# Lead of the first attention stage: fillers in halves between the half-steps, and the first shift of q built in the eleventh step in the fillers' PSUM

## Chip, cores and metric

The kernel runs on one core of a Trainium2 chip. The metric is the device time of one execution in microseconds (us); lower is better. All arithmetic is in f32. In the profiles one f32 matmul of the program shows as two hardware passes ("x8" for four matmuls), and so it is counted here.

## The reference, cut to what matters

The program is a block of an adaptive transformer: a 16-head attention with a gate and a position field, a soft mixture of 64 experts, and two layers of local attention and gated feed-forward. The change touches only the beginning of the first part, on x of shape (2, 1024, 256):

```python
def _L0_cond_ref(x, consciousness_state, ...):
    qkv = (x @ Wqkv.T + bqkv).reshape(Bb, Ss, 3, H, HD).transpose(2, 0, 3, 1, 4)   # H=16 heads of HD=16
    q, k, v = (qkv[0], qkv[1], qkv[2])
    attn = jax.nn.softmax(jnp.einsum('bhid,bhjd->bhij', q, k) / jnp.sqrt(jnp.float32(HD)), axis=-1)
    coh = jax.nn.sigmoid(jnp.tanh(comb @ Wc1.T + bc1) @ Wc2.T + bc2).transpose(0, 2, 1)
    mod = attn * coh[..., None]
    mod = mod / (mod.sum(-1, keepdims=True) + 1e-08)
    fp = _layernorm(jax.nn.relu(consciousness_state @ We1.T + be1) @ We2.T + be2, ln_g, ln_b)
    fa = jax.nn.softmax(jnp.einsum('be,se->bs', fp, pe), axis=-1)
    mod = (1.0 - fi) * mod + fi * fa[:, None, :, None]
    out = jnp.einsum('bhij,bhjd->bhid', mod, v).transpose(0, 2, 1, 3).reshape(Bb, Ss, Ee)
    return out @ Wout.T + bout
```

`comb` is x with the 64 state values joined to it. The softmax over the keys needs a maximum for each query and head before the exponentials.

## The kernel before, in words

The first attention is cut into eight units, each one batch and four heads. Each head has its own strip of 32 partitions (16 for the head, one more for the shift by the maximum), so that one matmul of a head contracts over 32 rows of TensorE's array and the four heads of a unit lie on its four row strips. A unit has 16 steps.

`maxima(step, half)` (L286 to L302) serves one block of 128 queries and one half of 512 keys for two of the four heads: two matmuls (L295; four passes of "32*128 32x512") write a PSUM tile `pm` of 128x1024, and VectorE reduces it to two maxima per query (L302). `half` 0 uses the row strips 0 and 1, `half` 1 the strips 2 and 3. `pm` comes from `wide`, a PSUM pool of two tiles, so a `pm` must wait until the reduction two half-steps earlier has read its tile. `largest(hu)` (L304) joins the two key halves of eight steps; `shift(hu)` (L308) transposes these maxima into PSUM (`pmx`, four transposes at L313) and adds them to q on VectorE, which gives `qs` (L317). `score` (L329) multiplies `qs` with the keys, and ScalarE takes the exponentials (L337).

The maxima run 12 steps ahead of the scores (`LEAD = 12`). So before the first score there is a lead of 12 steps with maxima alone, written out by hand (L661 to L699) for the queues of TensorE, VectorE and ScalarE: what stands first in the code stands first in each of these queues. To have work for TensorE beside VectorE's reductions, each step of the lead ends with a "filler", some other work of the stage that needs all 128 rows of the array: the input side of the coherence gate (`coherence_in`, L524, tiles `pz`, four passes a step), the values (`values`, L194, `pv`, eight passes of 256 columns), the logits of the field (`field_logits`, L615, `fl`), a rotation matrix (`rotation`, L652, `prot`) and the output of the gate (`coherence_out`, L542, `pc`, column strips of 32). Four very small ones go with them: `field_in`, `field_mean`, `field_var` and `field_out` (tiles `pfp`, `pfm`, `pfv`, `pfac`). [...] VectorE, ScalarE and GpSimd each read the fillers' results in passing.

A step of the lead is `maxima(m, 0)`, `maxima(m, 1)`, then the whole filler. After the twelfth step come `shift(0)`, in the PSUM of the maxima, and then the loop over scores, where each step pairs scores on two strips with maxima on the other two.

Of the kernel before, what the change touches and what calls it, by code (L numbers as in the profile page):

```python
# [17 lines left out]
P = 128  # L18
B = 2
S = 1024  # L20
D = 256
# [42 lines left out]
W_PRO, N_PRO = _layout([("wc1x", D), ("we2", D), ("wc2", 32)])  # L64
# [27 lines left out]
def tile_kernel(ctx: ExitStack, tc: tile.TileContext, a: dict, out: bass.AP):  # L92
    nc = tc.nc
# [24 lines left out]
    rot = res.tile([P, 2, D], F32, name="rot")  # L118
# [56 lines left out]
    def wide(name):  # L175
        return ps_s.tile([P, 2, 512], F32, tag="s", name=name)

    def pair(name):
        return ps_t[0].tile([P, 2, 512], F32, tag="t", name=name)
# [3 lines left out]

    pvs = {}

    def values(b, half, tile, part, lead=False):

        if part == 0:
            pvs[b, half] = tile("pv").rearrange("p x (y d) -> p (x y) d", d=D)
        pt = pvs[b, half]  # L190
        for y in (2 * part, 2 * part + 1):
            j = 4 * half + y
            for k in range(2):
                nc.tensor.matmul(  # L194
                    pt[:, y, :],
                    xT[b][:, k, j * P : (j + 1) * P],
                    watt("wv", k, 0, D),
                    start=(k == 0),
                    stop=(k == 1),
                )  # L200
        if part == 0:
            return
        to = v[b][:, 4 * half : 4 * half + 4, 0 : H0 * VW].rearrange("p j (h d) -> p j h d", d=VW)[
            :, :, :, 0:HD0
        ]
        pt = pt.rearrange("p j (h d) -> p j h d", d=HD0)
        bias = bcast(rows[:, ROWS["bv"]].rearrange("p (h d) -> p h d", d=HD0), 1, 4)
        if lead:
            nc.scalar.copy(to, pt)
            nc.gpsimd.tensor_tensor(to, to, bias, ALU.add)  # L210
        else:
            nc.vector.tensor_tensor(to, pt, bias, ALU.add)
# [66 lines left out]
    def spread(u):  # L279

        for what, dst in (("k", km[u % 3]), ("q", qm[u % 2])):
            for h in range(4):
                r0 = 64 * (u % 2) + HD0 * h
                nc.sync.dma_start(dst[32 * h : 32 * h + HD0, :], heads[what][r0 : r0 + HD0, :])
# [20 lines left out]
        mx2 = mxs.pop(hu)  # L305
        nc.vector.tensor_tensor(mxt[hu % 2][:, :, :, AUG], mx2[:, :, :, 0], mx2[:, :, :, 1], ALU.max)

    def shift(hu):  # L308

        u, n = divmod(hu, 2)  # L310
        pt = wide("pmx")[:, 0, :]
        for i in range(4):
            nc.tensor.transpose(  # L313
                pt[:, i * P : (i + 1) * P], mxt[hu % 2][:, i, :, :].rearrange("p h r -> p (h r)"), ident
            )
        at = slice(n * 512, (n + 1) * 512)
        nc.vector.tensor_tensor(qs[u % 2][:, at], qm[u % 2][:, at], pt, ALU.add)  # L317
# [131 lines left out]
    with tc.tile_pool(name="pro", bufs=1, side="right") as pro:  # L449
        w_cs = pro.tile([CD, N_CS], F32, name="w_cs")  # L450
        nc.gpsimd.dma_start(w_cs, a["w_cs"])
        w_pro = pro.tile([P, 2, N_PRO], F32, name="w_pro")
# [7 lines left out]
        def wsl(w, lay, name, c, lo, n):  # L460
            at = lay[name].start + lo
            return w[:, c, at : at + n]
# [43 lines left out]
        th = {}  # L506
# [8 lines left out]
                nc.vector.tensor_scalar(csb[:, c, :], pt[:, 0, c, :], col("bc1", c), None, ALU.add)  # L515
                nc.vector.tensor_scalar(hid[:, c, :], pt[:, 1, c, :], col("be1", c), 0.0, ALU.add, ALU.max)

        def coherence_in(b, n, c):
            if c == 0:
                th[b, n] = pair("pz")  # L520
            pz = th[b, n]
            t0 = n * 512
            for k in range(2):
                nc.tensor.matmul(  # L524
                    pz[:, c, :],
                    wsl(w_pro, W_PRO, "wc1x", k, c * P, P),
                    xT[b][:, k, t0 : t0 + 512],
                    start=(k == 0),
                    stop=(k == 1),
                )  # L530
            if c == 0:
                return
            th[b, n] = at2.tile([P, 2, 512], F32, tag="e", name="th", bufs=6)
            for c in range(2):
                nc.scalar.activation(th[b, n][:, c, :], pz[:, c, :], AF.Tanh, bias=csb[:, c, b : b + 1])

        def coherence_out():

            pc = pair("pc")[:, 0, :]
            for k in range(2):  # L540
                for g in range(4):
                    nc.tensor.matmul(  # L542
                        pc[32 * g : 32 * g + 32, :],
                        wsl(w_pro, W_PRO, "wc2", k, 0, 32),
                        th[g // 2, g % 2][:, k, :],
                        start=(k == 0),
                        stop=(k == 1),
                    )
            for g in range(4):
                th.pop((g // 2, g % 2))  # L550
            th["out"] = at2.tile([P, 2, 512], F32, tag="e", name="cg", bufs=6)[:, 0, :]
            nc.scalar.copy(th["out"], pc)

# [53 lines left out]
                    fpc[:, c, :], fpc[:, c, :], col("ln_g", c), col("ln_b", c), ALU.mult, ALU.add  # L607
                )

        def field_logits(n):  # L610
            if n == 0:
                th["fl"] = pair("fl")
            fl = th["fl"][0:B]
            for k in range(2):
                nc.tensor.matmul(  # L615
                    fl[:, n, :],
                    fpc[:, k, :],
                    peT[:, k, n * 512 : (n + 1) * 512],
                    start=(k == 0),
                    stop=(k == 1),  # L620
                )
            if n == 0:
                return
            th.pop("fl")
            fmx = pro.tile([B, 1], F32, name="fmx")
            nc.vector.tensor_reduce(fmx, fl.rearrange("p n t -> p (n t)"), AX.X, ALU.max)
            nc.vector.tensor_scalar(fmx, fmx, -1.0, None, ALU.mult)
            fe = at2.tile([P, 2, 512], F32, tag="e", name="fe", bufs=6)[0:B].rearrange("p n t -> p (n t)")
            fsum = pro.tile([B, 1], F32, name="fsum")
            nc.scalar.activation(  # L630
                fe, fl.rearrange("p n t -> p (n t)"), AF.Exp, bias=fmx, accum_out=fsum
            )
            th["fe"] = fe, fsum
# [11 lines left out]
                nc.tensor.transpose(pt[:, i, :], fe[:, i * P : (i + 1) * P], ident[0:B, 0:B])  # L645
            nc.vector.tensor_copy(fac.rearrange("p (b i) -> p i b", b=B), pt)

        def rotation(mats):
            pt = pair("prot")
            for c in range(2):  # L650
                for k in range(2):
                    nc.tensor.matmul(  # L652
                        pt[:, c, :D],
                        mats[0][:, k, c * P : (c + 1) * P],
                        mats[1][:, k, :],
                        start=(k == 0),
                        stop=(k == 1),
                    )
            nc.scalar.copy(rot, pt[:, :, :D])

        with tc.manual_schedule(  # L661
            engines={mybir.EngineType.PE, mybir.EngineType.DVE, mybir.EngineType.Activation}
        ):
            pq, pk = wide("pqk"), wide("pqk")
            for pt, what, n in ((pq, "q", 0), (pk, "k", 0), (pk, "k", 1), (pq, "q", 1)):
                project_part(pt, 0, what, 0, n)
            project_end(pk, "k", 0)
            project_end(pq, "q", 0)
            spread(0)
            from_state()  # L670
            coherence_in(0, 0, 0)
            coherence_in(0, 0, 1)
            values(0, 0, pair, 0, True)
            values(0, 0, pair, 1, True)
            fill = [
                [field_in, lambda: coherence_in(0, 1, 0)],
                [field_mean, lambda: coherence_in(0, 1, 1)],
                [field_var, lambda: values(0, 1, pair, 0, True)],
                [lambda: values(0, 1, pair, 1, True), lambda: spread(1)],
                [lambda: field_logits(0)],  # L680
                [lambda: field_logits(1)],
                [lambda: coherence_in(1, 0, 0)],
                [lambda: coherence_in(1, 0, 1), field_scale],
                [lambda: coherence_in(1, 1, 0)],
                [lambda: coherence_in(1, 1, 1), field_out],
                [lambda: rotation(mats)],
                [coherence_out],
            ]
            mats = None
            for m in range(LEAD):  # L690
                maxima(m, 0)
                maxima(m, 1)
                for f in fill[m]:
                    f()
                if m == 3:
                    mats = matrices()
                if m == 8:
                    largest(0)
            shift(0)  # L699

    def of_banks(bufs):
        banks.close()
# [11 lines left out]
    for u in range(len(units)):  # L714
        if u % 2 == 0 and u + 2 < len(units):
            b, g = units[u + 2]
# [29 lines left out]
    with tc.manual_schedule(  # L746
        engines={mybir.EngineType.PE, mybir.EngineType.DVE, mybir.EngineType.Activation}
    ):
        for s in range(STEPS):
# [11 lines left out]
            m = s + LEAD  # L761
# [204 lines left out]
    y = [mo1.tile([P, NE // 4, D], F32, name="y0"), xp.tile([P, NE // 4, D], F32, tag="y1", name="y1")]  # L966
    dxs = ExitStack()
    dx = dxs.enter_context(tc.tile_pool(name="dx", bufs=2))
    with tc.manual_schedule(
# [5 lines left out]
        for it in range(3, ITS):  # L975
            n, m = divmod(it, 8)
# [6 lines left out]
            i = it - ITS + 8  # L983
# [89 lines left out]
    with tc.manual_schedule(  # L1073
# [250 lines left out]
        def halves(f):  # L1324
            l, b, t0 = chunk(f)
            nc.gpsimd.tensor_tensor(
                fa["sq"][:, 0, :], shifted(xb, 0, b, t0, 512), shifted(xb, 1, b, t0, 512), ALU.add
            )
# [343 lines left out]
```

## Time and profile before

| what | us |
|---|---|
| median of 3 runs (1624.53 to 1625.74) | 1625.15 |
| the profiled execution | 1625.17 |
| its span, first to last instruction | 1623.2 |
| TensorE's busy time in the span | 1591.8 |
| mean granted TensorE clock | 0.999 of full speed |
| the lead: first maxima to first score, from 24.65 to 67.19 | 42.5 |
| one reduction of a `pm` (L302), mean of 256 | 1.220 |

A page of the profile gives busy times per engine and the costliest groups of instructions. Three views go closer. The timeline lists instructions by start, merged where one form follows itself. The chain of waits follows the end of a stretch back, at each step to what released it, so its pieces lie end to end. A table of windows gives each engine's busy time in a stretch. PE is a matmul pass, PEld the loading of its weights, DVE is VectorE, ACT is ScalarE, POOL is GpSimd.

### The profile page before, as it was taken

The page shows a single profiled execution, that of the slowest core. Times are in us where ns is not written, and L with a number is a line of the kernel's source. Part 1 is how long each engine was busy: PE and PEld are TensorE (multiplying, and loading weights), DVE is VectorE, ACT ScalarE, POOL GpSimd, SP SyncE. Part 2 cuts the span into 40 slices and gives each one's busy share as a digit, 9 for nine tenths or more (in the row PEclk, how much of TensorE's full clock was granted, in tenths as well). Part 3 has the DMA queues.
Part 4 walks back from the last instruction along what each step waited for, and adds up shares of the span by engine and source line. Part 5 has one row for each costly group of instructions (what it writes and reads, how often), then busy time and mean ns, then how long its engine had stood idle before and what let it go on. Part 6 is the DMA issues. An engine that isn't in the chain of part 4 may idle for free.

```text
span 1623.2 us, 22628 instructions
## 1 busy us (share of the span) xinstructions
PE 1591.8 (98%) x8660; PEld 803.4 (49%) x8660; DVE 941.9 (58%) x1605; ACT 884.8 (55%) x1653; POOL 538.3 (33%) x830
## 2 busy tenths in 40 slices
PE   8999999999999999999999999999999999999998
PEld 4333333333333444444877676555555555655543
DVE  4768758776763122225446755757576666666632
ACT  2477767777886222235234544656657575656531
POOL 3233323333330100000103434555565555465411
PEclk9999999999999999999999999999999999999999
DMA  5100000010000544546532002000100001000001
GB/s 157 52 14 14 1 16 12 1 21 8 1 1 27 169 141 151 178 148 195 184 126 78 27 1 80 1 1 1 65 1 0 14 1 54 1 6 22 14 14 39
DMA packets 49707, 82.65 MB, mean 51 GB/s; under 512 B 4536, under 2 KB 24928, under 8 KB 49344
## 3 DMA queue, kind: packets, MB, share of 16 engines
q1 hardware_dynamic: 47056, 75.38, 15.0%
q0 software_dynamic: 1584, 5.29, 1.1%
q8 instruction: 68, 1.11, 0.3%
q10 hardware_dynamic: 960, 0.56, 0.1%
q14 instruction: 39, 0.32, 0.1%
HBM read 56.04 MB, written 20.97 MB: 47 GB/s over the span
## 4 chain that ended last, share of the span: by engine, by line
PE 89%; DVE 6%; ACT 2%; POOL 1%; issue 1%; DMA 1%; DVEq 0%; ACTq 0%; POOLq 0%
PE pga L1371 8%; PE sc L329 8%; PE po L347 7%; PE pm L295 7%; PE lg L795 7%; PE sl L821 7%; PE pq L1121 6%; PE cmb L909 5%; PE pwo L1310 3%; PE po L1290 3%; PE sc L1210 3%; PE py L1396 3%; PE pv L1177 3%; PE pe L1271 3%; PE pqk L265 2%; PE py L842 2%
## 5 line engine op out<-in xcount | busy, mean ns | idle before, releaser
L302 DVE TENSOR_REDUCE mx<-pm 128x2 f32<-128x1024 f32 x256 | 302.5, 1220 | 117.9 <-PE pm L295 117.3
L337 ACT ACTIVATE e<-sc 128x512 f32<-128x512 f32 (+1 forms) x500 | 266.2, 611 | 72.2 <-PE pm L295 44.6
L329 PE MATMUL sc<-qs,km 32*128 32x512 f32 x1024 | 254.7, 619 | 0.9 <-DVE qs L317 0.9
L295 PE MATMUL pm<-km,qm 32*128 32x512 f32 x1024 | 246.0, 619 | 2.4 <-ACT xa L432 0.6
L365 POOL TENSOR_TENSOR ob<-ob,part 128x512 f32<-128x512 f32 x101 | 128.4, 1271 | 270.2 <-ACT part L364 270.2
L1227 DVE CUSTOM_DVE_ANT_0 e<-sc,mask,zn 128x256 f32<-128x256 f32 (+1 forms) x256 | 102.3, 463 | 69.5 <-PE sc L1210 69.5
L1371 PE MATMUL pga<-hc,w 128*128 128x512 f32 x320 | 141.1, 593 | 0.0
L1260 POOL TENSOR_SCALAR e<-e,den 128x256 f32<-128x256 f32 (+1 forms) x128 | 131.1, 1038 | 27.0 <-DVE den L1256 27.0
L347 PE MATMUL po<-e,v 128*32 128x512 f32 x1024 | 136.7, 604 | 0.0
L329 PEld LDWEIGHTS sc<-qs,km 32*128 32x128 f32 x1024 | 87.5, 183 | 84.6 <-ACT e L337 64.4
L1244 ACT ACTIVATE e<-e,nmx 128x256 f32<-128x256 f32 (+1 forms) x256 | 123.5, 485 | 1.9 <-DVE nmx L1227 1.6
L1145 POOL TENSOR_TENSOR t<-raw,tabs 128x512 f32<-128x512 f32 x64 | 81.5, 1295 | 124.8 <-ACT raw L1135 119.6
L1121 PE MATMUL pq<-wqo,xa 128*128 128x512 f32 x256 | 115.9, 595 | 1.6 <-DVE xb L897 0.9
L909 PE MATMUL cmb<-xb,y 128*128 128x256 f32 x512 | 116.6, 380 | 0.2 <-ACT xb L895 0.2
L795 PE MATMUL lg<-phi,xa 128*128 128x512 f32 x256 | 115.9, 595 | 0.3 <-ACT xa L432 0.3
L821 PE MATMUL sl<-dsp,xb 128*128 128x512 f32 x256 | 114.9, 592 | 0.0
L295 PEld LDWEIGHTS pm<-km,qm 32*128 32x128 f32 x1024 | 82.8, 183 | 60.0 <-DVE mx L302 31.7
L805 DVE TENSOR_TENSOR l<-lg,keep 128x512 f32<-128x512 f32 x32 | 22.1, 692 | 143.5 <-ACT keep L803 143.5
L909 PEld LDWEIGHTS cmb<-xb,y 128*128 128x128 f32 x512 | 94.9, 190 | 16.6 <-issue 3.2
L1135 ACT COPY raw<-pq 128x1024 f32<-128x1024 f32 x32 | 32.4, 1013 | 128.6 <-PE pq L1121 126.8
L1371 PEld LDWEIGHTS pga<-hc,w 128*128 128x128 f32 x320 | 59.2, 190 | 67.2 <-issue 63.9
L803 ACT COPY keep<-lg 128x512 f32<-128x512 f32 x32 | 18.7, 585 | 125.1 <-issue 107.4
(212 smaller groups left out, 2491.2 us busy)
## 6 DMA issues: line engine op xcount, KB each, us to landing
lgd<-keep SPq DMA_DIRECT2D x64, 256.0 KB, 2.4
w<-in_ffn_W SPq DMA_DIRECT2D x16, 1024.0 KB, 7.5
ebig<-lgd SPq DMA_DIRECT2D x64, 256.0 KB, 3.3
wqo<-in_wqkv SPq DMA_DIRECT2D x2, 1536.0 KB, 8.6
w<-in_w SPq DMA_DIRECT2D x2, 1386.0 KB, 5.9
km<-hk SPq DMA_DIRECT2D x32, 64.0 KB, 2.3
qm<-hq SPq DMA_DIRECT2D x32, 64.0 KB, 2.3
phi<-in_phi SPq DMA_DIRECT2D x1, 2048.0 KB, 7.6
```

The costliest lines, as they stand in the source:

```text
L295: nc.tensor.matmul(pm[:, x, :], qm[u % 2][r, i * P : (i + 1) * P], km[u % 3][r, n * 512 : (n + 1) * 512], start=True, stop=True,)
L302: nc.vector.tensor_reduce(mxs[hu][:, i % 4, 2 * half : 2 * half + 2, n], pm, AX.X, ALU.max)
L329: nc.tensor.matmul(sc[:, x, :] if both else sc[x], km[u % 3][r, j * P : (j + 1) * P], qs[u % 2][r, n * 512 : (n + 1) * 512], start=True, s ...
L337: nc.scalar.activation(part, t, AF.Exp, scale=1.0 / HD0**0.5)
L347: nc.tensor.matmul(po[32 * hh : 32 * hh + 32, :], v[b][:, j, at : at + 32], es[s, hh // 2][:, hh % 2, :], start=True, stop=True,)
L365: nc.gpsimd.tensor_tensor(obs[u, n], obs[u, n], part, ALU.add)
L795: nc.tensor.matmul(lg[:, b, :], xa[:, k, b, 1 + m * P : 1 + (m + 1) * P], phi[:, k, n * 512 : (n + 1) * 512], start=(k == 0), stop=(k == 1),)
L821: nc.tensor.matmul(accs[n][b][:, c, :], xo_tm[:, b * 8 + m, c * P : (c + 1) * P], d[:, b, :], start=(m == 0), stop=(m == 7),)
L909: nc.tensor.matmul(acs[q][:, c, :], y[b][:, 4 * jj + j, c * P : (c + 1) * P], eT[:, j // 2, j % 2 * 256 : (j % 2 + 1) * 256], start=(jj == ...
L1121: nc.tensor.matmul(pq[:, x, :], shifted(xa, k, b, w * WIN, P), load["wqkv"][:, k, x * 512 : (x + 1) * 512], start=(k == 0), stop=(k == 1),)
L1260: engine.tensor_scalar(e[:, x, c, lo:], e[:, x, c, lo:], den[:, x, c : c + 1], None, ALU.mult)
L1371: nc.tensor.matmul(pt[:, x, :], load["w1"][:, k, lo : lo + P], hcs[f][:, k, :], start=(k == 0), stop=(k == 1))
```

## The change

Each filler is cut in two, and a half stands behind each `maxima` of a step: `maxima(m, 0)`, first half, `maxima(m, 1)`, second half. No matmul, reduction or transfer is added or left out. The small fillers stay with the same step: `field_in`, `field_mean` and `field_var` now between the step's first maxima and its first half of filler, `field_out`, `field_scale` and the loads of the second unit behind the second half. `shift(0)` goes from the end of the lead to the end of the eleventh step (index 10) and takes its PSUM tile from `pair`. `coherence_out`, the filler of the last step, keeps its tile in `th["pc"]` between its halves. The queues of SP and GpSimd keep their order; on TensorE and VectorE only the lead changes.

```diff
-    def values(b, half, tile, part, lead=False):
+    def values(b, half, tile, part, lead=False, which=(0, 1)):
...
-        for y in (2 * part, 2 * part + 1):
+        for y in (2 * part + i for i in which):
...
-    def shift(hu):
+    def shift(hu, tile=wide):
...
-        pt = wide("pmx")[:, 0, :]
+        pt = tile("pmx")[:, 0, :]
...
-        def coherence_in(b, n, c):
-            if c == 0:
+        def coherence_in(b, n, c, which=(0, 1)):
+            if c == 0 and 0 in which:
                 th[b, n] = pair("pz")
...
-            for k in range(2):
+            for k in which:
...
-            if c == 0:
+            if c == 0 or 1 not in which:
                 return
...
-        def coherence_out():
-
-            pc = pair("pc")[:, 0, :]
-            for k in range(2):
-                for g in range(4):
+        def coherence_out(k):
+
+            if k == 0:
+                th["pc"] = pair("pc")[:, 0, :]
+            pc = th["pc"]
+            for g in range(4):
...
+            def halves(f, *args):
+                return [lambda y=y: f(*args, (y,)) for y in range(2)]
+
+            def value_halves(half, part):
+                return [lambda y=y: values(0, half, pair, part, True, (y,)) for y in range(2)]
+
             fill = [
...
+                halves(coherence_in, 0, 1, 0),
+                halves(coherence_in, 0, 1, 1),
+                value_halves(1, 0),
+                value_halves(1, 1),
+                halves(field_logits, 0),
+                halves(field_logits, 1),
+                halves(coherence_in, 1, 0, 0),
+                halves(coherence_in, 1, 0, 1),
+                halves(coherence_in, 1, 1, 0),
+                halves(coherence_in, 1, 1, 1),
+                [lambda: rotation(0), lambda: rotation(1)],
+                [lambda: coherence_out(0), lambda: coherence_out(1)],
             ]
-            mats = None
+            also = {
+                (0, 0): field_in,
+                (1, 0): field_mean,
+                (2, 0): field_var,
+                (3, 1): lambda: spread(1),
+                (7, 1): field_scale,
+                (9, 1): field_out,
+                (10, 1): lambda: shift(0, pair),
+            }
             for m in range(LEAD):
-                maxima(m, 0)
-                maxima(m, 1)
-                for f in fill[m]:
-                    f()
+                for y in range(2):
+                    maxima(m, y)
+                    early = (m, y) in ((0, 0), (1, 0), (2, 0))
+                    if early:
+                        also[m, y]()
+                    fill[m][y]()
+                    if (m, y) in also and not early:
+                        also[m, y]()
                 if m == 3:
                     mats = matrices()
                 if m == 8:
                     largest(0)
-            shift(0)
```

`field_logits` and `rotation` are cut in the same way.

More of the change, by code (lines that the diff above doesn't have):

```diff
@@ L184, in tile_kernel @@
     pvs = {}
-    def values(b, half, tile, part, lead=False):
-        if part == 0:
+    def values(b, half, tile, part, lead=False, which=(0, 1)):
+        if part == 0 and 0 in which:
             pvs[b, half] = tile("pv").rearrange("p x (y d) -> p (x y) d", d=D)
         pt = pvs[b, half]
-        for y in (2 * part, 2 * part + 1):
+        for y in (2 * part + i for i in which):
             j = 4 * half + y
@@ L200, in values @@
                 )
-        if part == 0:
+        if part == 0 or which == (0,):
             return
@@ L535, in coherence_in @@
                 nc.scalar.activation(th[b, n][:, c, :], pz[:, c, :], AF.Tanh, bias=csb[:, c, b : b + 1])
-        def coherence_out():
-            pc = pair("pc")[:, 0, :]
-            for k in range(2):
-                for g in range(4):
[L542 to L548, printed above, removed]
+        def coherence_out(k):
[3 more added lines that the diff above has]
+            for g in range(4):
+                nc.tensor.matmul(
+                    pc[32 * g : 32 * g + 32, :],
+                    wsl(w_pro, W_PRO, "wc2", k, 0, 32),
+                    th[g // 2, g % 2][:, k, :],
+                    start=(k == 0),
+                    stop=(k == 1),
+                )
+            if k == 0:
+                return
             for g in range(4):
                 th.pop((g // 2, g % 2))
+            th.pop("pc")
             th["out"] = at2.tile([P, 2, 512], F32, tag="e", name="cg", bufs=6)[:, 0, :]
@@ L608, in field_var, with field_logits @@
                 )
-        def field_logits(n):
-            if n == 0:
+        def field_logits(n, which):
+            if n == 0 and 0 in which:
                 th["fl"] = pair("fl")
             fl = th["fl"][0:B]
-            for k in range(2):
+            for k in which:
                 nc.tensor.matmul(
@@ L621, in field_logits @@
                 )
-            if n == 0:
+            if n == 0 or 1 not in which:
                 return
@@ L646, in field_out, with rotation @@
             nc.vector.tensor_copy(fac.rearrange("p (b i) -> p i b", b=B), pt)
[L648 to L659, printed above, removed]
+        def rotation(c):
+            if c == 0:
+                th["rot"] = pair("prot")
+            pt = th["rot"]
+            for k in range(2):
+                nc.tensor.matmul(
+                    pt[:, c, :D],
+                    mats[0][:, k, c * P : (c + 1) * P],
+                    mats[1][:, k, :],
+                    start=(k == 0),
+                    stop=(k == 1),
+                )
+            if c == 1:
+                nc.scalar.copy(rot, pt[:, :, :D])
         with tc.manual_schedule(
@@ L674, in tile_kernel @@
             values(0, 0, pair, 1, True)
+            def halves(f, *args):
+                return [lambda y=y: f(*args, (y,)) for y in range(2)]
+            def value_halves(half, part):
+                return [lambda y=y: values(0, half, pair, part, True, (y,)) for y in range(2)]
             fill = [
[L676 to L687, printed above, removed]
-            ]
-            mats = None
-            for m in range(LEAD):
-                maxima(m, 0)
-                maxima(m, 1)
-                for f in fill[m]:
-                    f()
+                halves(coherence_in, 0, 1, 0),
```

## The prediction

> **What bounds the kernel now.** First the page, for which engine sets the end:
>
> ```profile
> PE 1591.8 (98%) x8660; PEld 803.4 (49%) x8660; DVE 941.9 (58%) x1605; ACT 884.8 (55%) x1653; POOL 538.3 (33%) x830
> ...
> PE 89%; DVE 6%; ACT 2%; POOL 1%; issue 1%; DMA 1%; DVEq 0%; ACTq 0%; POOLq 0%
> ```
>
> The second line is the chain that ended last: 89% of it is TensorE. What lengthens or shortens TensorE's queue in the lead moves all behind it, unless some other engine was late there. So I looked at the lead alone, as a window, and then at the chain in it, whose pieces (start, us, what) lie end to end:
>
> ```profile
> 24.65:67.18 42.53, 41.66 (x197) 17.46 (x197) 31.35 (x38) 12.24 (x17) 15.11 (x38) 1.00 0.06 11
> ```
>
> ```profile
> 35.62 1.07 PE pm L295 x8
> ...
> 45.06 1.65 PE pm L295 x8
> 46.71 1.91 PE pz L524 x4
> 48.62 1.64 PE pm L295 x8
> 50.27 1.91 PE pz L524 x4
> 52.18 1.09 PE pm L295 x8
> 53.27 1.91 PE pz L524 x4
> ...
> 65.73 0.60 PE pmx L313 x4
> 66.33 0.02 issue
> 66.35 0.70 DVE qs L317
> 67.05 0.14 issue
> 67.19 0.70 PE sc L329 x2
> ```
>
> The lead is TensorE's alone, at full clock (1.00), with VectorE busy 31.35 of 42.53 us. A step is one piece of maxima and one of filler. The eight maxima passes of a step take 1.03 to 1.21 us in seven steps and about 1.65 in five; the timeline shows both kinds:
>
> ```profile
> 38.54 1.72 PE L295 MATMUL pm<-km,qm 32*128 32x512 f32 x8
> 38.65 1.01 ACT L209 COPY v<-pv 128x1024 f32<-128x1024 f32 x1 [3.55 <-PE pv L194]
> 39.13 0.30 PEld L295 LDWEIGHTS pm<-km,qm 32*128 32x128 f32 x4 [0.29 <-DVE mx L302]
> 39.72 2.36 DVE L302 TENSOR_REDUCE mx<-pm 128x2 f32<-128x1024 f32 x2 [0.64 <-PE pm L295]
> 40.19 0.09 PEld L615 LDWEIGHTS fl<-peT,fpc 128*2 128x2 f32 x2 [0.76 <-issue]
> 40.19 1.88 PE L615 MATMUL fl<-peT,fpc 128*2 128x512 f32 x4
> 40.62 0.08 PEld L615 LDWEIGHTS fl<-peT,fpc 128*2 128x2 f32 x1 [0.34 <-issue]
> 41.05 0.09 PEld L615 LDWEIGHTS fl<-peT,fpc 128*2 128x2 f32 x1 [0.34 <-issue]
> 42.00 1.26 PE L295 MATMUL pm<-km,qm 32*128 32x512 f32 x8
> ```
>
> At 38.54 the first half runs alone; the second waits for a reduction until 39.13, and the filler starts at 40.19. A half alone on two row strips so holds the array 40.19 - 39.13 = 1.06 us. At 35.62 the chain has both halves, on four strips, in 1.07. Two halves side by side cost what one does. That decides the case.
>
> **The change, part by part.** The twelve maxima pieces of the chain are 1.07, 1.07, 1.21, 1.07, 1.65, 1.19, 1.65, 1.64, 1.09, 1.64, 1.03 and 1.67, together 15.98.
>
> Removed: the wait of the second half for a reduction. Without it twelve pieces would be 12 x 1.07 = 12.84, so 15.98 - 12.84 = 3.1 us can be won. It is all won, I think: a reduction begins 39.72 - 38.54 = 1.18 after its half-step's start and takes 1.22, so its tile is free at 2.4; the half that needs it comes two half-steps later, at 4.0 to 4.2 (below). This 1.6 us of slack also covers what else stands on VectorE between: the maximum over `fl` (1.20) with its sign (0.14), and `qs` (0.69).
>
> Added: a filler stands between the halves, and it takes all 128 rows, so they no longer share the array. 24 halves x 1.06 = 25.4 in place of 12.84: +12.6.
>
> Added: cutting a filler. The `pz` loads start at 46.64 and 47.18, the passes in the middle follow by 0.43, and the next `pm` starts 0.52 after the last pass begins (1.91 = 0.53 + 0.43 + 0.43 + 0.52). A half is 0.53 + 0.52 = 1.05, so a cut `pz` is 2.10, +0.19, six times. `fl` has 0.43 and 0.52 (40.19, 40.62, 41.05, 42.00): 2 x 0.95 against 1.81, +0.09, twice. `pv` and `prot` are eight passes of half the length in 1.92; less four inner passes of 0.215 a half is 1.06, +0.20, three times. `pc`, 1.85 with inner passes of 0.43, gives halves of 0.98 or 0.99, +0.1, once. Sum 1.14 + 0.18 + 0.60 + 0.10 = +2.0. The small fillers keep their passes: 0.
>
> Moved: the shift. Before, its way to the first score is 65.73 to 67.19, 1.46 us. After, the four transposes stay on the path between two full-height fillers and a `pm`: the same kind at 75.82 (`pct`) takes 0.58 to the next score. The addition on VectorE then hides behind the last step's 4 us (without that cover 0.70). But the first score also needs the PSUM that the gate's output is copied from: that copy, started 0.14 after `pc`'s end (65.66 to 65.80), takes 0.59 and the score follows by 0.14: 0.87. Now it is last. 0.58 + 0.87 - 1.46 = 0.0. Putting the shift earlier only lets ScalarE's copy take its place.
>
> PSUM of the fillers: `pmx` takes the tile of the last `pz`, read by ScalarE's tanh a full step earlier, and `pc` that of `prot`, whose copy (0.59) lies under the transposes and a maxima half (1.6). The tightest is `pv` in step 3: tanh ended 1.38 after its filler (31.96 to 33.34), and `pv` now comes 1.06 + 0.47 = 1.53 after it: 0.15 spare. I take 0; if it misses, some 0.1. No DMA moves: the loads of the second unit stay behind step 4's filler, and SP and GpSimd keep their order.
>
> Behind the lead: the first two steps of the score loop take 71.89 - 67.19 = 4.70 to the first output product, two later ones without it 2 x (2.93 - 1.0) = 3.86 (2.93 is 79.47 to 82.40 to 85.33). This ramp of 0.84 bounds what a different start could give back or, as much again, cost: -0.8 to +0.8; I take 0, since score and maxima there still run on opposite strips.
>
> Sum: -3.1 + 12.6 + 2.0 + 0.0 = +11.5; the passes follow each other by some hundredths less at best (1.05 for 1.06 is -0.2), so +11.3. A step is then 2 x (1.06 + 1.05) = 4.2 us against 3.0 to 3.6. The profiled execution's 1625.17 is its span of 1623.2 and 1.97 outside it, which nothing here touches; it stands 0.02 above the median. So 1636.5.
>
> [...] The row says that the lead's matmuls were busy 41.66 of 42.53 us, which leaves 0.87 to win; by the pieces 3.1 were waited. [...] By the busy share the sum would be +13.7 instead of +11.5.
>
> [...] In the rows a switch between strips and full height shows as 0.53 and 0.52 in place of 0.43. [...]
>
> **Rivals.**
>
> *The array overlaps modes* (not slower). If a half's second pass ran under the filler's first, each of 24 halves would hide 0.43: 11.3 - 10.3 = +1.0, 1626.2, no change. For it: in the chain `pm` starts 0.52 after `pfac` began, before that eighth small pass was done. Against: `pfac` contracts over 2 rows, on one strip; behind every half the 128-row filler starts 0.52 after the last pass. It decides from the point where a filler's load starts within 0.1 of the half's second pass. 4%.
>
> *The loop behind gives some back.* The whole ramp of 0.84, 0.2 of hundredths and the shift's 0.75 in full: 1634.7. For it: the score loop starts with VectorE less behind. Against: score pairs and ScalarE set that ramp, not VectorE. 10%.
>
> *A new wait.* Halves leave less between a filler's parts and its readers; if every half of maxima waited as the late ones did before (1.65 - 1.07 = 0.58) in half the steps, twice a step, 12 x 0.58 = +7: 1643.5; with a few only, 1638. Against: the slack of 1.6 and 0.15 above. 6%.
>
> **How the numbers follow.** The forecast, 80%: 1636.5, by itself 1635 to 1638. Down to 1633.5 the second rival lies inside, up to 1639 part of the third. About 0.2%, 3.3 us, is what a measurement tells from no change. Slower by more (over 1628.4) holds the forecast, the second and third rivals: 0.96. The first gives no change, 0.03, and 0.01 for faster, where the cut costs nothing too.
>
> **What would show it.** Right: in the chain of the lead, `pm` pieces of four passes of about 1.06, 24 of them, each followed by half a filler of about 1.05 (0.95 for `fl`); the lead some 54 us long; no idle of TensorE for L302 in it; the first score waiting for the copy of `pc` (`cg`) rather than for `qs`. The stretch from first score to end as before, within 0.8. Wrong: halves of 0.6 us, or four-strip groups still, or a lead under 45 us.

## The result, and the profile after

| | before | after |
|---|---|---|
| median of runs, us | 1625.45 (4 runs) | 1635.45 (4 runs, 1635.08 to 1637.29) |
| ratio, 95% interval | | 1.0066 [1.0053, 1.0079] |
| timed again, 21 and 5 runs | 1625.07 | 1635.45, ratio 1.0069 [1.0056, 1.0082] |
| the profiled execution: time, span | 1625.17, 1623.2 | 1637.29, 1635.3 |
| the lead, first maxima to first score | 42.53 | 53.70 |

The change makes the kernel slower by about 10 us, 0.6 to 0.7% (the ratios given lie a little above the quotients of the medians, 1.0062 and 1.0064). The lead alone is 11.17 us longer. The page of the kernel after has the same shares as before, and more matmul time:

```profile
PE 1604.7 (98%) x8660; PEld 804.8 (49%) x8660; DVE 943.0 (58%) x1605; ACT 884.8 (54%) x1653; POOL 538.1 (33%) x830
...
PE 89%; DVE 6%; ACT 2%; POOL 1%; issue 1%; DMA 1%; DVEq 0%; ACTq 0%; POOLq 0%
```

TensorE's busy time rose by 12.9 us with the same 8660 matmul passes, and the lead is busy from end to end, as the window over it shows (columns: window, length, then busy time and count of PE, PEld, DVE, ACT, POOL, then the clock, the busy share of the DMA engines and GB/s):

```profile
24.29:77.99 53.70, 52.99 (x198) 18.25 (x197) 32.59 (x38) 12.23 (x17) 15.12 (x38) 1.00 0.04 7
```

A reader who goes by busy shares would call this lead full. But 25.4 of the 53.7 us are now maxima on two of the four row strips, with the other two idle. The chain of waits in it (start, us, what) shows the steps that stood at 45.06 to 55 before, and the end:

```profile
51.11 1.06 PE pm L295 x4
52.16 1.06 PE pz L524 x2
53.22 1.06 PE pm L295 x4
54.28 1.06 PE pz L524 x2
55.33 1.06 PE pm L295 x4
56.39 1.05 PE pz L524 x2
...
72.74 0.44 PE pmx L313 x4
73.18 1.06 PE pm L295 x4
74.23 1.00 PE pc L543 x8
75.23 1.06 PE pm L295 x4
76.29 1.04 PE pc L543 x8
77.33 0.02 issue
77.35 0.59 ACT cg L556
77.94 0.04 issue
77.99 0.70 PE sc L329 x2
```

Before, the eight maxima passes of a step stood in one piece of 1.03 to 1.67; now four passes take 1.06 (1.03 once, behind `pfac`), and there are two such pieces a step. No piece is longer: the wait for VectorE is gone. At the end ScalarE's copy `cg` stands where VectorE's `qs` stood.

### The profile page after: what moved, and what is told of

Its sections match the earlier page's. It is cut to its first block, busy times and chain, and to the rows that moved or that the text cites. A ratio compares the mean times of both kernels' runs of the same rounds, so it can differ in the third digit from the quotient of the medians.

```text
span 1635.3 us, 22629 instructions
## 1 busy us (share of the span) xinstructions
PE 1604.7 (98%) x8660; PEld 804.8 (49%) x8660; DVE 943.0 (58%) x1605; ACT 884.8 (54%) x1653; POOL 538.1 (33%) x830
## 4 chain that ended last, share of the span: by engine, by line
PE 89%; DVE 6%; ACT 2%; POOL 1%; issue 1%; DMA 1%; DVEq 0%; ACTq 0%; POOLq 0%
PE pga L1395 8%; PE sc L329 8%; PE pm L295 7%; PE po L347 7%; PE lg L819 7%; PE sl L845 7%; PE pq L1145 6%; PE cmb L933 5%; PE pwo L1334 3%; PE po L1314 3%; PE sc L1234 3%; PE pv L1201 3%; PE py L1420 3%; PE pe L1295 3%; PE pqk L265 2%; PE py L866 2%
## 5 line engine op out<-in xcount | busy, mean ns | idle before, releaser
L295 PE MATMUL pm<-km,qm 32*128 32x512 f32 x1024 | 256.2, 619 | 2.4 <-ACT xa L432 0.6
```

The costliest lines, as they stand in the source:

```text
L295: nc.tensor.matmul(pm[:, x, :], qm[u % 2][r, i * P : (i + 1) * P], km[u % 3][r, n * 512 : (n + 1) * 512], start=True, stop=True,)
```

## The experiments

**The change again.**

> The changed kernel as it is, timed again beside the kernel before. The lead in its trace (first maxima to first score) is 11.2 us longer than before. Theory A, all of it reaches the end: median 11.0 to 11.4 above the kernel before, ratio 1.0068 to 1.0070. Theory B, about 1 us of it is given back behind the lead or ahead of it: ratio 1.0062 or less, and the stretch from the first score to the last instruction is then 1 us shorter than the 1556.0 of before in a trace whose clock shows nothing.

The median was 1635.45 against 1625.07: 10.4 us more, short of theory A's 11.0 to 11.4 and above what theory B allows. The interval of the ratio, 1.0069 [1.0056, 1.0082], holds both theories, so the times do not decide between them. The lead was 53.70 once more. The traces speak against B: from the first score to the last matmul's start they have 1550.7 us before and 1552.0 in both traces of the changed kernel, longer and not shorter. In both the extra 1.3 comes in one place, and it is a matter of the clock; the start of the lead varies too, in kernels that are the same up to it (last section).

**Only the sharing of the array.**

```diff
             for m in range(LEAD):
-                maxima(m, 0)
-                maxima(m, 1)
+                for w in (m - m % 2, m - m % 2 + 1):
+                    maxima(w, m % 2)
                 for f in fill[m]:
```

> Fillers whole and as many changes between strips and full height as in the kernel before, but the two half-steps that stand next to each other are those of two steps on the same two row strips instead of one step's on opposite strips. Theory (the loss is the lost sharing of the array): a group of eight maxima passes takes 0.53 + 0.43 + 0.43 + 0.52 = 1.9 us, twelve of them 22.9 in place of 16.0; lead 49.4 to 49.6, time +6.9 to +7.1. Rival (the loss of the change comes from the changes of mode and the cuts): lead no longer than before, 39.4 to 42.5, time -3 to 0.

Measured: 1632.38, +7.3 us, ratio 1.0044 [1.0028, 1.0059]; lead 49.5. Its chain:

```profile
50.07 1.91 PE pz L524 x4
51.98 1.92 PE pm L295 x8
53.90 1.91 PE pz L524 x4
55.81 1.92 PE pm L295 x8
57.73 1.91 PE pz L524 x4
```

Eight passes on two strips take 1.92, where eight on four strips took 1.07; the fillers, uncut, are the 1.91 of before. So the lost sharing alone, with the wait won, makes 7.0 of the 11.2 us.

**Only the halves.** The changed kernel with `shift(0)` again behind the lead:

```diff
-                (10, 1): lambda: shift(0, pair),
...
                     largest(0)
+            shift(0)
```

> The change without the moved shift: fillers in halves, the shift behind the lead in the PSUM of the maxima as before. Theory: the maxima and fillers cost what they do in the changed kernel, the way behind the last filler is again about 1.5 us; 24 pieces of four maxima passes of 1.06; lead 53.7 - 0.44 (no transposes in it) + 0.8 (the longer way at its end) = 54.0 to 54.2, time +11.4 to +11.7. Rival (the moved shift makes part of the loss): lead under 53.4.

Measured: lead 54.01, as expected, and 0.3 longer than with the shift moved: the move is a small gain in the change, not part of its loss. The time was 1635.97, +10.7, ratio 1.0067 [1.0053, 1.0081]; the +11.4 to +11.7 lie inside the interval, but 0.3 us is below what it can tell. The 4.5 us between this lead and the 49.5 of the run with the same strips is what the further switches and the cuts cost.

**Only the shift.**

```diff
-    def shift(hu):
+    def shift(hu, tile=wide):
...
-        pt = wide("pmx")[:, 0, :]
+        pt = tile("pmx")[:, 0, :]
...
-                [lambda: rotation(mats)],
+                [lambda: rotation(mats), lambda: shift(0, pair)],
...
-            shift(0)
```

> The kernel before with the shift alone moved behind the rotation in the eleventh step, in the fillers' PSUM; fillers whole. Theory (the copy of the gate's output takes its place): the way from the end of the gate's matmuls to the first score falls from 1.53 to about 0.8, the transposes cost 0.45 to 0.58 further up: lead 42.2 to 42.5, time -0.3 to 0. Rival (the shift's 1.46 was all on the path and is now hidden): lead 41.0 to 41.3, time -1.2 to -1.5. Rival (the move is part of the loss): +0.5 or more.

Measured: 1624.36, ratio 0.9998 [0.9989, 1.0007], no change that can be told; lead 41.79, 0.74 less. None of the three expectations named that. The chain shows what I had left out:

```profile
61.06 0.44 PE pmx L313 x4
61.49 1.23 PE pm L295 x8
62.73 1.90 PE pc L542 x16
64.62 0.02 issue
64.65 0.59 ACT cg L552
65.24 0.04 issue
65.28 0.70 PE sc L329 x2
```

The last piece of maxima is 1.23, before it was 1.67. The transposes (0.44) stand ahead of a half that would have waited 0.44 longer for VectorE, so in this kernel they are free. In the changed kernel nothing waits there, and they cost their 0.44. That is the difference between the 0.74 won here and the 0.31 won there (54.01 to 53.70).

**Cutting every second step.**

```diff
                 for y in range(2):
-                    maxima(m, y)
+                    if m % 2:
+                        maxima(m, y)
+                    elif y == 0:
+                        maxima(m, 0)
+                        maxima(m, 1)
```

> The changed kernel, but in every second step (the 1st, 3rd, to the 11th) both maxima come first and both filler halves after them, uncut in effect; only six steps are cut. Theory (each cut step loses 1.05 of shared array and 0.1 to 0.2 for the cut, whatever the waits): lead 53.7 - 6 x 1.05 - 1.1 = 46.3, no wait of the maxima for VectorE in it, time +3.6 to +4.0. Rival (a few cuts are enough to win the waits and cost little): lead 42.5 or less, time 0 or below.

Measured: 1630.07, +4.8, ratio 1.0030 [1.0018, 1.0041]; lead 47.75. The rival falls, but the lead is 1.4 longer than I expected, and the chain shows a wait that I had ruled out:

```profile
38.41 1.06 PE pm L295 x4
39.47 1.06 PE pv L194 x4
40.53 1.39 PE pm L295 x8
41.92 1.81 PE fl L619 x4
43.73 1.06 PE pm L295 x4
```

1.39 in place of 1.07. The second half in the group at 40.53 needs the tile of the lone half at 38.41, only 2.1 us earlier, and a tile is free 2.4 us after its half-step's start. So TensorE waits 0.32 to 0.43 us in four of the six whole steps, 1.4 together. The slack that makes the fully cut lead free of waits comes from its slowness: the half that needs a tile comes two half-steps of 2.1 later.

**The wait removed in another way.** Here the fillers stay whole. All their PSUM tiles, still from one pool of two, have one bank each (128x512, half of `pair`'s 128x1024), and the two banks so freed are a third tile for the maxima. For that `values` copies its result per two blocks, and `coherence_in` takes its tanh after each step and not after every second. The shift is moved as in the change.

```diff
+    ps_x = banks.enter_context(tc.tile_pool(name="ps_x", bufs=1, space=PSUM))
...
+    def third(name):
+        return ps_x.tile([P, 2, 512], F32, tag="x", name=name)
+    def solo(name):
+        return ps_t[0].tile([P, 1, 512], F32, tag="t", name=name)
...
-                maxima(m, 0)
-                maxima(m, 1)
+                for y in range(2):
+                    tile = wide
+                    if m not in (4, 5, 6, 7):
+                        calls += 1
+                        tile = third if calls % 3 == 0 else wide
+                    maxima(m, y, tile)
```

> The kernel before with the wait taken away in another way: fillers whole, their PSUM tiles of one bank each, and the two banks so freed are a third tile for the maxima in steps 1 to 4 and 9 to 12 (the field's logits hold them in between); the shift is moved as in the change. Theory (the wait of the second half is a wait for a free tile, and only that): eight maxima passes in 1.07 in those eight steps, 1.07 or 1.65 in the other four; lead 39.8 to 40.6, time -1.9 to -2.7. Rival (VectorE's reductions or ScalarE's smaller copies set the pace): lead 42 or more, time 0 or above.

Measured: 1623.43, ratio 0.9991 [0.9982, 0.9999]; lead 40.89. Eight steps have 1.03 to 1.07, the four without the third tile 1.65, 1.19, 1.65 and 1.64. The mechanism held; the lead is 0.3 above my range, because I had counted on fewer waits in those four. The median fell by 1.6, less than the expected 1.9 to 2.7, which the interval does not exclude. Against the run with the shift alone (41.79) the third tile shortens the lead by 0.9.

Then the third tile in all twelve steps, with the field's logits in one-bank tiles that ScalarE copies to SBUF (the edit is shown against the run just told):

```diff
+            fl = solo("fl")[0:B, 0, :]
...
+            nc.scalar.copy(fe[:, n, :], fl)
...
-                    tile = wide
-                    if m not in (4, 5, 6, 7):
-                        calls += 1
-                        tile = third if calls % 3 == 0 else wide
-                    maxima(m, y, tile)
+                    calls += 1
+                    maxima(m, y, third if calls % 3 == 0 else wide)
```

> The kernel with a third tile for the maxima, now in all twelve steps: the field's logits go through one-bank tiles and are copied to SBUF by ScalarE. Theory (what is left of the wait is that for a tile): twelve pieces of eight passes of 1.03 to 1.07, none of 1.65; lead 40.8 - 1.8 = 38.9 to 39.2, time -3.2 to -3.8 against the kernel before, ratio 0.9977 to 0.9980. Rival (at 3 us a step VectorE or ScalarE fall behind, with two more copies of 0.6 each): lead 40.5 or more.

```profile
41.11 1.07 PE pm L310 x8
42.18 1.81 PE fl L627 x4
43.99 1.07 PE pm L310 x8
45.06 1.92 PE pz L539 x4
46.97 1.35 PE pm L310 x8
48.33 1.91 PE pz L539 x4
50.24 1.07 PE pm L310 x8
```

Measured: 1622.96 against 1625.23, ratio 0.9982 [0.9973, 0.9991]. The interval holds the expected 0.9977 to 0.9980, but the median fell by 2.3 and not by 3.2 to 3.8. The kernel has the shortest lead and the lowest median here; the 0.5 us between its median and that of the run before are less than the intervals can tell. The lead is 39.34, 3.2 less than before. Eleven pieces are 1.03 to 1.07. One of 1.35 is left, and the timeline names it: at 44.63 VectorE reduces the logits for 1.21 us, just when the next maxima come in.

```profile
43.92 1.14 PE L310 MATMUL pm<-km,qm 32*128 32x512 f32 x8
44.02 0.57 ACT L634 COPY fe<-fl 2x512 f32<-2x512 f32 x1 [2.31 <-PE fl L627]
44.63 1.21 DVE L639 TENSOR_REDUCE fmx<-fe 2x1 f32<-2x1024 f32 x1
```

So the rival is right in one step of twelve, and the lead misses my range by 0.14.

## Why the prediction was right

*The bound.* TensorE's queue in the lead sets what follows. Matched matmul by matmul, the changed kernel runs behind the first score within 0.03 us of the one before for 830 us (in its second trace within 0.11). Nothing was given back or lost in the score loop: the 0.84 of its ramp stayed as it was, and the second rival falls. The time alone would not have told: the median, 1635.45, is as near to that rival's 1634.7 as to 1636.5.

*The maxima.* Forecast -3.1 + 12.6 = +9.5; the 24 pieces, 25.41 together in place of 15.98, measure +9.4. Pieces of 1.06 show both halves of it: the wait is gone, and the array is not shared. The run with the same strips puts a price on the sharing without any cut.

*The cuts.* Forecast +2.0, with halves of 1.05, 0.95, 1.06 and 0.98; the chain has 1.06 (0.96 or 0.97 right behind the three small fillers of the first steps), 0.95, 1.06 and 1.00. With the shift left in place the lead was 11.48 longer, 9.43 of it maxima; that leaves +2.05 for the cuts.

*The shift.* Forecast 0.0, measured -0.3: the one term that was off. The transposes were put at 0.58 by the row of `pct`, and they took 0.44, with no score but a maxima pass behind them; the score followed `cg` by 0.04 instead of 0.14. That the copy would become last was right.

*Sum.* +9.4 + 2.0 - 0.3 is the 11.1 to 11.2 of the lead. The forecast's +11.3 was +11.5 less 0.2 for passes that would follow each other more closely. That 0.2 did not come, the pieces are 1.06; the shift gave 0.3 in its place. So the mechanism was right, and that 11.3 is within 0.2 of the lead owes something to luck. The medians moved by 10.0 and 10.4, about 1 us less than the lead; the interval of the ratio, 8.6 to 12.8 us, cannot tell that from 11.2. The profiled execution moved by 12.1. Its further 0.9 lies outside the lead: 1.3 of clock, less 0.36 because its maxima began at 24.29 and not at 24.65.

*The rivals.* Strips and full height do not overlap here: a filler starts 1.06 after its half of maxima began. The one overlap is that of before, maxima that start while the last small pass of `pfac` still runs. A new wait did not come in the changed kernel; it came where only half the steps were cut.

*The busy share.* By it 0.87 us of wait could be won; with the third tile everywhere the twelve maxima pieces sum to 13.08 in place of 15.98, 2.9 less, so the pieces were the better measure here. The busy share leaves out a wait that lies under passes of the other half: before, from 38.50 to 39.10, TensorE counts as busy for all of the 0.60 us, while the second half waits until 39.13.

A `pz` filler of 1.91 takes 2 x 1.06 when it is cut, so the further switches have a price, here 0.2 us for one filler; no run shows what in a switch takes the time. The two experiments divide the loss: they measured 7.0 us for the lost sharing and 4.5 for further switches and cuts, where the sum has 6.9 (22.9 - 16.0) and 4.5 (25.4 - 22.9 + 2.0).

## What to carry to other kernels

In this kernel matmuls on different row strips are cheap only beside each other: eight passes on four strips took 1.07 us, four on two strips 1.06. Before full-height work is put between such matmuls to fill a wait, compare the wait (here 3.1 us in all) with what the separation costs (here 14.6). The wait for a PSUM tile was better met by a further tile, here from two banks that came free when each filler's result was read step by step. And a piece that is moved into a stretch with waits may be free there and not in the version where these waits are gone, as the transposes were: free beside a wait of 0.44 us, 0.44 us without it.

## What the runs showed beside it

The granted clock is not the same in two executions of nearly the same work. Some 970 us behind the first score TensorE waits four times for GpSimd, 0.4 to 1.2 us each, and among these waits the clock falls to half (0.50 over the middle window after). Before and after, windows over the waits, the next values' projection and the next products (columns as above; the clock stands behind POOL):

```profile
1037.78:1041.60 3.82, 2.25 (x8) 1.57 (x9) 3.79 (x3) 0.98 (x1) 2.65 (x3) 0.74 0.00 0
1041.60:1044.11 2.51, 2.51 (x5) 0.87 (x4) 2.48 (x6) 1.01 (x1) 2.46 (x3) 0.72 0.00 0
1044.11:1045.14 1.03, 1.03 (x18) 0.85 (x17) 0.56 (x1) 0.59 (x1) 1.03 (x2) 1.00 0.00 0
```

```profile
1048.65:1052.48 3.83, 2.31 (x9) 1.58 (x9) 3.80 (x3) 0.98 (x1) 2.65 (x3) 0.64 0.00 0
1052.48:1056.03 3.55, 3.55 (x6) 1.01 (x5) 3.03 (x6) 1.01 (x1) 3.52 (x4) 0.50 0.00 0
1056.03:1057.28 1.25, 1.25 (x18) 1.08 (x17) 0.00 (x0) 0.59 (x1) 0.72 (x1) 0.80 0.00 0
```

The same work takes 2.51 + 1.03 = 3.54 us before and 3.55 + 1.25 = 4.80 after: the 1.26 us. The clock's record in the trace has one stretch at half clock of 3.41 us here before and one of 6.83 after. Over all nine traces, those with 3.41 take 1550.7 to 1551.2 us from the first score to the start of the last matmul (five), those with 6.83 1552.0 to 1552.5 (four). No run shows what sets these lengths.

The start varies as well, by up to 1.2 us: the first maxima begin at 23.45 to 24.65 us in the nine traces, though the matmuls ahead of them are the same. This too goes with the clock. In every trace the first passes follow each other by 0.85 us and the later ones by 0.43, and the clock's record begins, at full speed, where they change over: at 12.0 to 12.2 us in the four traces that begin the maxima after 24.2, at 10.4 to 10.5 us in the four that begin them before 23.6.

The timed runs point the same way: the 38 runs of the kernel before that were timed beside the experiments have spans of 1620.3 to 1623.2 us where the mean clock was 0.999 or more, and of 1623.1 to 1625.7 where it was 0.997 or less. That the timed runs of the changed kernel differ from the profiled ones for this reason is likely (the two profiled took 1637.3 and 1637.4, the seven others 1634.8 to 1635.8), but it was not shown.
